# One-hots in sets of four, a table stream released through ScalarE, and later passes in a graph layer on one core

## Chip, cores and metric

One NeuronCore of a Trainium2 chip. The time is device microseconds for one execution of the kernel; the median of three runs is given with the lowest and the highest.

## What is computed

A graph layer: 12500 nodes of 128 features, 200000 edges sorted by their destination, four edge types. The reference, cut to what matters:

```python
def _layernorm(x, axis=-1, eps=1e-05):
    m = jnp.mean(x, axis=axis, keepdims=True)
    v = jnp.var(x, axis=axis, keepdims=True)
    return (x - m) / jnp.sqrt(v + eps)
...
# for every edge e: h = relu(_layernorm(x))
# out = x + segment_sum over dst of (h[src[e]] @ W[type[e]] + b[type[e]])
```

The two comment lines put into words what the reference does with a loop over the four types. Destinations are drawn as 12500·u², so low node numbers have many edges and high ones few.

## The kernel before

**The table.** In the first 190 us the kernel loads `x` by spans, makes `h`, splits each value into three bf16 parts and writes them to `htab`, 12500 rows of 3 × 128 bf16, in DRAM (`first_part`, `second_part`, `third_part`). Edges are handled in chunks of 128. From then on there are two kinds of work, which share all engines.

**The sparse part.** 1003 chunks with few edges per destination are gathered: `gather` (L543) issues one indirect DMA per chunk from GpSimd, two chunks to a tile `hm` of the pool `rows` (18 buffers). VectorE makes a one-hot `oh` of destination and type for each chunk (L560); TensorE multiplies rows by one-hot, three matmuls a chunk (L577, `sum_up`), into a bank `ps` for four chunks; ScalarE evicts it as `sb` (L580). For each group of 16 chunks `weigh` (L595 to L604) applies the four matrices, and VectorE adds the result to a ring of output columns (L665), which is transposed and written out (L690 to L697).

**The dense part.** The first 512 chunks belong to a few thousand destinations with many edges. Here the kernel counts how often each source stands in the edges of each (destination, type) pair, and multiplies the whole table by the counts. Destinations come in *units* of three, their edges in *slots* of 128, 1167 slots in all; up to 27 units make a *batch*, 18 batches (`MANY`, `UB`).

- `count(vs, counts)`: for every slot VectorE makes two one-hots, `o1` (128 × 128, L947 or L951, source within a block, scaled so that the three destinations of a unit land in three bytes of one number) and `o2` (128 × 392, L952, block and type). TensorE multiplies them (L963) into a bank `pt` of `x_ps` (four buffers), and after the last slot of a unit ScalarE turns the bank into int32 `counts` (L966, 476 evictions). One-hots are made `AHEAD` = 8 slots ahead, in 12 buffers each.
- `multiply(vs, counts)`: reads the bytes of `counts` as fp8 numbers. SP streams the table, `HB` = 4 of its 98 columns (128 partitions × 384 bf16 each) to a load `hs` (L997, pool of 4 buffers, 25 loads a pass, 450 in all). For each column three matmuls, one for each part of `h`, accumulate in the bank `pa` (L1001, 294 a pass, 5292 in all), which has one buffer. After the last one ScalarE moves `pa` to `sd` (L1011), and `tail` applies the matrices (L1015).
- `dense_work()` runs `multiply` of batch n and `count` of batch n + 1 side by side: at each step the one with the least share done goes on, with `BEHIND` = 0.06 added to the pass. `pace()` says how much of the dense work stands beside each chunk of the sparse part.

**What sets the order.** From L1248 on the order of TensorE, VectorE and ScalarE is written out by hand (`tc.manual_schedule`): their instructions run in the order in which the Python program emits them. A tile that is taken again from its pool waits for the last reader of its buffer, by a semaphore of the reader's engine. SP and GpSimd issue their DMAs in their own order and wait, one after the other, for the buffer of each.

The main loop goes over groups of 16 chunks, and within one over `sum_up`'s steps; each step runs the dense work up to `pace`, then a share of the small VectorE jobs (`side`). `tails` are jobs that a pass leaves behind: `tail`, its additions, and `check_sums`, ten small VectorE instructions per batch that check the counts.

Of the kernel before, what the change touches and what calls it, by code (L numbers as in the profile page):

```python
# [35 lines left out]
F32 = mybir.dt.float32  # L36
BF16 = mybir.dt.bfloat16
# [11 lines left out]
P = 128  # L49
# [6 lines left out]
C0 = 512  # L56
UB = 27
MANY = 16
HB = 4
AHEAD = 8  # L60
HOTS = AHEAD + 4
BEHIND = 0.06
RING = 2048
OT = 4
HG = 2
# [8 lines left out]
def kernel(  # L74
# [449 lines left out]
    def gather_raw(k, by):  # L524
# [9 lines left out]
                held_by(one, by, "rows of x come while the table is made, spread over its blocks")  # L534
        return hm

    def gather(t0, g):
        got = []
        for h0 in range(0, g, HG):
            hm = hpool.tile([P, HG * D3], BF16, name="hm")  # L540
            for i in range(h0, min(h0 + HG, g)):
                at = (t0 + i) % (TURN * P)
                one = nc.gpsimd.indirect_dma_start(  # L543
                    out=hm[:, (i - h0) * D3 : (i - h0 + 1) * D3],
                    out_offset=None,
                    in_=htab,
                    in_offset=bass.IndirectOffsetOnAxis(ap=srcf[:, at : at + 1], axis=0),
                )
# [19 lines left out]
    def sum_up(t0, g, rows, oh, last):  # L568
        win = window_of(C0 + t0)
        K = NT * win  # L570
        sb = spool.tile([P, G * KM], F32, name="sb")[:, : G * K].rearrange("p (g t n) -> p g t n", g=G, t=NT)
        for i0 in range(0, g, SG):
            i1 = min(i0 + SG, g)
            ps = s_ps.tile([P, 512], F32, name="ps")[:, : SG * K].rearrange("p (i n) -> p i n", i=SG)
            for i in range(i0, i1):
                for c in range(3):
                    nc.tensor.matmul(ps[:, i - i0, :], rows(i, c), oh[:, i, :], start=(c == 0), stop=(c == 2))  # L577
                if i % HG and i + 1 < i1:
                    yield (i + 1) / g
            nc.scalar.copy(sb[:, i0:i1].rearrange("p g t n -> p g (t n)"), ps[:, : i1 - i0, :])  # L580
            yield i1 / g

        finish.append(weigh(t0, g, oh, sb, last))
# [348 lines left out]
            nc.scalar.copy(acc[:, a:z], pn[:, : z - a])  # L932


    def count(vs, counts):
        todo = []
        for i, u in enumerate(vs):
            of = slots_of(u)
            todo += [(i, c, by, n == 0, n == len(of) - 1) for n, (c, by) in enumerate(of)]
        made = {}  # L940

        def make(k):
            i, s, by, first, last = todo[k]
# [8 lines left out]
            nc.vector.tensor_scalar(o2[:, :NB], iota_n, hkT[:, s : s + 1], None, ALU.is_equal)  # L952
            made[k] = o1, o2

        done = 0
        for k, (i, s, by, first, last) in enumerate(todo):
            while done < min(k + 1 + AHEAD, len(todo)):
                make(done)
                done += 1
            o1, o2 = made.pop(k)  # L960
            if first:
                pb = x_ps.tile([P, NB + NT], F32, name="pt")
            nc.tensor.matmul(pb, o1, o2, start=first, stop=last)  # L963
            if last:

                nc.scalar.copy(counts[:, :, i * NT : (i + 1) * NT], pb.rearrange("p (b t) -> p b t", t=NT))  # L966
            yield (k + 1) / len(todo)
        def check_sums():
            n = len(vs)
            bi = sdp.tile([P, UB], I32, name="bi")  # L970
            nc.vector.tensor_copy(bi[:, :n], counts[:, NW, : n * NT].rearrange("p (i t) -> p i t", t=NT)[:, :, 0])
            bb = sdp.tile([P, 3, UB], I32, name="bb")
            nc.vector.tensor_single_scalar(bb[:, 0, :n], bi[:, :n], 255, op=ALU.bitwise_and)
            nc.vector.tensor_single_scalar(bb[:, 2, :n], bi[:, :n], 16, op=ALU.arith_shift_right)
            nc.vector.tensor_single_scalar(bi[:, :n], bi[:, :n], 8, op=ALU.arith_shift_right)
            nc.vector.tensor_single_scalar(bb[:, 1, :n], bi[:, :n], 255, op=ALU.bitwise_and)
            bf = sdp.tile([P, 3, UB], F32, name="bf")
            nc.vector.tensor_copy(bf[:, :, :n], bb[:, :, :n])
            top = sdp.tile([P, 2], F32, name="top")
            nc.vector.tensor_reduce(top[:, 0:1], bf[:, :, :n], AX.XY, ALU.max)  # L980
            nc.vector.tensor_reduce(top[:, 1:2], bf[:, :, :n], AX.XY, ALU.add)
            nc.vector.tensor_max(most, most, top[:, 0:1])
            nc.vector.tensor_add(held, held, top[:, 1:2])

        tails.append(check_sums)

    tails = []

    def multiply(vs, counts):
        nu = len(vs)  # L990
# [3 lines left out]
        for j0 in range(0, NW, HB):  # L994
            j1 = min(j0 + HB, NW)
            hs = hsp.tile([P, HB, D3], BF16, name="hs")
            nc.sync.dma_start(hs[:, : j1 - j0, :], htab.rearrange("(p j) f -> p j f", j=NW)[:, j0:j1, :])  # L997
            for j in range(j0, j1):
                of = counts[:, j, : nu * NT * 4].rearrange("p (v m) -> p m v", m=4)[:, :3, :]
                for c in range(3):  # L1000
# [246 lines left out]
    o2s = op2.tile([P, HOTS, NB + NT], BF16, name="o2")  # L1247
    nc.vector.memset(o2s[:, :, NB:], 1.0)  # L1248
# [23 lines left out]
    for gi, (t0, g) in list(enumerate(zip(starts, sizes)))[RAW:]:  # L1272
# [16 lines left out]
        for j, part in enumerate(sum_up(t0, g, *now, gi >= FULL)):  # L1289
# [27 lines left out]
        if work is None and not dense_out:  # L1317
            while tails:
                tails.pop(0)()
            dense_out = True  # L1320
            assert goes[0] < gi

# [161 lines left out]
```

## Time and profile before

| | us |
|---|---|
| median of 3 runs | 1678.33 |
| lowest, highest | 1674.64, 1681.06 |
| profiled execution | 1684.81 |
| its span in the profile | 1683.1 |

The profile is of one execution. Engines: PE is TensorE's matmul, PEld its weight load, which overlaps; DVE is VectorE, ACT ScalarE, POOL GpSimd, SP SyncE (SPq is its DMA queue). Lines such as L963 are lines of the kernel. A group of instructions is shown as line, engine, operation, output <- inputs and count, then busy time and the mean ns of one, then idle time of the engine ahead of it and what ended most of that. The chain is followed back from the last instruction to what released each step; "issue" in it is time in which the engine waited for nothing that the profile shows. The waits' columns are the time in total (us), the times, and the longest. The timeline and the chain in order of time give start (us), duration (us) and what ran. The stretches give the length, then busy us and the number of instructions for each engine, the clock that TensorE was granted, the share of the DMA engines and GB/s.

### The profile page before, as it was taken

The page shows a single profiled execution, that of the slowest core. Times are in us where ns is not written, and L with a number is a line of the kernel's source. Part 1 is how long each engine was busy: PE and PEld are TensorE (multiplying, and loading weights), DVE is VectorE, ACT ScalarE, POOL GpSimd, SP SyncE. Part 2 cuts the span into 40 slices and gives each one's busy share as a digit, 9 for nine tenths or more (in the row PEclk, how much of TensorE's full clock was granted, in tenths as well). Part 3 has the DMA queues.
Part 4 walks back from the last instruction along what each step waited for, and adds up shares of the span by engine and source line. Part 5 has one row for each costly group of instructions (what it writes and reads, how often), then busy time and mean ns, then how long its engine had stood idle before and what let it go on. Part 6 is the DMA issues. An engine that isn't in the chain of part 4 may idle for free.

```text
span 1683.1 us, 32652 instructions
## 1 busy us (share of the span) xinstructions
PE 1420.6 (84%) x10984; PEld 926.8 (55%) x10984; DVE 1033.9 (61%) x5305; ACT 445.3 (26%) x1095; POOL 1026.0 (61%) x1078
## 2 busy tenths in 40 slices
PE   3768589898889988888989888988888988898885
PEld 1336366555565556555656555655555555565554
DVE  7880677665766566576647566656654756565244
ACT  5593231222212122212221222122222222222111
POOL 7436666666666566666665666666656666666561
PEclk9875699999999999999999999999999999999997
DMA  7543376766666666666666666666656666666662
GB/s 225 158 155 82 88 233 207 205 199 193 201 190 194 190 196 191 203 193 183 197 194 183 185 196 183 191 201 187 188 165 193 203 187 191 181 194 186 198 185 68
DMA packets 157498, 308.92 MB, mean 184 GB/s; under 512 B 28202, under 2 KB 81116, under 8 KB 157325
## 3 DMA queue, kind: packets, MB, share of 16 engines
q1 hardware_dynamic: 107645, 204.99, 40.3%
q0 software_dynamic: 49680, 101.81, 21.3%
q8 instruction: 86, 1.41, 0.4%
q14 instruction: 87, 0.71, 0.1%
HBM read 290.65 MB, written 16.04 MB: 182 GB/s over the span
## 4 chain that ended last, share of the span: by engine, by line
PE 77%; issue 10%; DVE 5%; another core or an unknown queue 3%; ACT 2%; DMA 2%; SPq 1%; DVEq 0%; ACTq 0%
PE pa L1001 45%; PE pt L963 12%; PE ps L577 7%; PE py L604 6%; PE pt L1015 1%; DMA hs<-htab 1%; PE ps L634 1%; PE py L595 1%; PE pt L690 1%; DVE stt L439 1%; ACT h L460 1%; DVE o L952 1%; DMA hm<-in_x_dram 1%; DVE oh L560 1%
## 5 line engine op out<-in xcount | busy, mean ns | idle before, releaser
L543 POOL DMA_INDIRECT hm<-htab,srcT x1003 | 970.2, 967 | 580.3 <-issue 225.4
L1001 PE MATMUL pa<-counts,hs 128*128 128x324 fp8e4 (+1 forms) x5292 | 976.1, 305 | 112.9 <-issue 95.8
L1001 PEld LDWEIGHTS <-hs 128*128 128x128 bf16 x5292 | 494.2, 97 | 396.0 <-issue 167.9
L963 PE MATMUL pt<-o,o 128*128 128x396 bf16 x1167 | 383.5, 338 | 45.8 <-issue 39.1
L952 DVE TENSOR_SCALAR o<-iota_n,hkT 128x392 bf16<-128x392 f16 x1167 | 386.2, 331 | 14.0 <-PE pa L1001 5.5
L966 ACT CAST counts<-pt 128x396 int32<-128x396 f32 x476 | 229.4, 494 | 506.5 <-PE pt L963 204.4
L560 DVE TENSOR_SCALAR oh<-iota_b,keyT 128x56 bf16<-128x56 bf16 (+8 forms) x1003 | 169.3, 259 | 265.4 <-PE pt L963 88.1
L580 ACT COPY sb<-ps 128x224 f32<-128x224 f32 (+8 forms) x251 | 99.6, 397 | 531.2 <-PE pt L963 182.9
L665 DVE TENSOR_TENSOR ring<-ring,py 128x14 f32 (+7 forms) x976 | 167.5, 172 | 102.5 <-issue 21.5
L577 PE MATMUL ps<-oh,hm 128*128 128x56 bf16 (+8 forms) x3009 | 192.2, 197 | 29.3 <-issue 28.6
L951 DVE TENSOR_SCALAR o<-iota,loT 128x128 bf16<-128x128 bf16 x644 | 169.7, 264 | 75.2 <-PE pt L963 27.8
L577 PEld LDWEIGHTS <-hm 128*128 128x128 bf16 x3009 | 164.7, 98 | 89.5 <-issue 43.7
L951 DVE TENSOR_SCALAR o<-iota,loT,byT 128x128 bf16<-128x128 bf16 x417 | 136.1, 326 | 81.4 <-PE pt L963 40.9
L963 PEld LDWEIGHTS <-o 128*128 128x128 bf16 x1167 | 113.2, 98 | 95.3 <-issue 43.8
L604 PE MATMUL py<-sb,wsb 128*128 128x224 f32 (+7 forms) x488 | 128.6, 404 | 3.5 <-issue 3.2
L604 PEld LDWEIGHTS py<-sb,wsb 128*128 128x128 f32 x488 | 87.3, 191 | 28.5 <-issue 6.8
L527 POOL DMA_INDIRECT hx<-in_x_dram,srcT x48 | 50.2, 1045 | 39.4 <-DVE stt L439 13.9
L599 ACT CAST cnt<-py 128x224 bf16<-128x224 f32 (+7 forms) x61 | 24.0, 394 | 96.4 <-PE pt L963 29.2
L460 ACT ACTIVATE h<-hm,nmrt,rstdt 128x128 f32<-128x128 f32 x98 | 42.8, 495 | 3.5 <-DMA hm<-in_x_dram 2.6
L489 PE MATMUL ps<-h,ident 128*128 128x384 f32 (+1 forms) x34 | 18.1, 618 | 17.7 <-ACT h L460 14.6
L947 DVE TENSOR_SCALAR o<-iota,loT 128x128 bf16<-128x128 bf16 x106 | 26.8, 253 | 8.5 <-remote 4.2
L1015 PE MATMUL pt<-sd,wsb 128*128 128x81 f32 (+1 forms) x144 | 25.4, 334 | 2.7 <-ACT sd L1011 2.7
(234 smaller groups left out, 623.2 us busy)
## 6 DMA issues: line engine op xcount, KB each, us to landing
hs<-htab SPq DMA_DIRECT2D x432, 384.0 KB
hm<-htab,srcT POOLq DMA_INDIRECT x1003
htab<-h SPq DMA_DIRECT2D x32, 288.0 KB
xo<-in_x_dram SPq DMA_DIRECT2D x23, 256.0 KB
out_dram<-xo SPq DMA_DIRECT2D x23, 256.0 KB
hm<-in_x_dram SPq DMA_DIRECT2D x18, 192.0 KB
hs<-htab SPq DMA_DIRECT2D x18, 192.0 KB
hm<-in_x_dram SPq DMA_DIRECT2D x14, 168.0 KB
```

Source lines behind the costliest of these rows:

```text
L460: return nc.scalar.activation(h, xt(k), AF.Relu, bias=nmr[:, k : k + 1], scale=rstd[:, k : k + 1]).ins
L543: one = nc.gpsimd.indirect_dma_start(out=hm[:, (i - h0) * D3 : (i - h0 + 1) * D3], out_offset=None, in_=htab, in_offset=bass.IndirectOffse ...
L560: nc.vector.tensor_scalar(oh[:, i, :], iota_b[:, :K], keyf[:, at : at + 1], None, ALU.is_equal)
L577: nc.tensor.matmul(ps[:, i - i0, :], rows(i, c), oh[:, i, :], start=(c == 0), stop=(c == 2))
L580: nc.scalar.copy(sb[:, i0:i1].rearrange("p g t n -> p g (t n)"), ps[:, : i1 - i0, :])
L604: nc.tensor.matmul(py[:, :g, :], wsb[:, t, :], sb[:, :g, t, :], start=False, stop=(t == NT - 1))
L665: nc.vector.tensor_tensor(to, to, of(i), ALU.add)
L951: nc.vector.tensor_scalar(o1, iota_1, loT[:, s : s + 1], by, ALU.is_equal, ALU.mult)
L952: nc.vector.tensor_scalar(o2[:, :NB], iota_n, hkT[:, s : s + 1], None, ALU.is_equal)
L963: nc.tensor.matmul(pb, o1, o2, start=first, stop=last)
L966: nc.scalar.copy(counts[:, :, i * NT : (i + 1) * NT], pb.rearrange("p (b t) -> p b t", t=NT))
L1001: nc.tensor.matmul(pa[:, : 3 * nu * NT].rearrange("p (m v) -> p m v", m=3), hs[:, j - j0, c * D : (c + 1) * D], of, start=(j == 0 and c == 0),
```

## The change

- `HB` 4 → 5: 98 columns make 20 loads a pass, 360 in all, of 491,520 bytes for 393,216; `hs` has 3 buffers for 4 (`STREAM`).
- A load of `hs` no longer waits for the matmul that last read its buffer. It waits for the first eviction of counts (ScalarE) that was emitted after that matmul, if there is one by then (`left_at`, `by_blocks`); otherwise for the matmul as before.
- One-hots in sets of four slots (`SLOTS`), four sets in all (`SETS`). The first one-hot of a set waits for the last counting matmul of the set four before; the first counting matmul of a set waits for the set's last one-hot. `o2` is made ahead of `o1`. Two sets are complete, and the next one grows by one slot per counting matmul.
- `BEHIND` 0.06 → 0.15.
- The pool `rows` has 16 buffers for 18, and a gather waits until all buffers of its block of four chunks have been read (`readers`, `BLOCK`).
- `check_sums` does one of its steps per chunk of the sparse part and no longer all in one place.

The diff, cut to its core:

```diff
@@ -56,10 +56,13 @@
 C0 = 512
 UB = 27
 MANY = 16
-HB = 4
-AHEAD = 8
-HOTS = AHEAD + 4
-BEHIND = 0.06
+HB = 5
+SLOTS = 4
+SETS = 4
+STREAM = 3
+ROWS = 16
+BLOCK = 4
+BEHIND = 0.15
 RING = 2048
 OT = 4
 HG = 2
@@ -230,7 +233,7 @@
     flag = const.tile([P, 1], I32, name="flag")
 
     mid = ExitStack()
-    hpool = mid.enter_context(tc.tile_pool(name="rows", bufs=18))
+    hpool = mid.enter_context(tc.tile_pool(name="rows", bufs=ROWS))
     opool = mid.enter_context(tc.tile_pool(name="onehots", bufs=2))
     spool = mid.enter_context(tc.tile_pool(name="typed", bufs=2))
     x_ps = mid.enter_context(tc.tile_pool(name="x_ps", bufs=4, space=PSUM))
@@ -534,10 +537,15 @@
                 held_by(one, by, "rows of x come while the table is made, spread over its blocks")
         return hm
 
+    taken = [0]
+    readers = []
+
     def gather(t0, g):
         got = []
         for h0 in range(0, g, HG):
             hm = hpool.tile([P, HG * D3], BF16, name="hm")
+            taken[0] += 1
+            left = taken[0] + (min(h0 // BLOCK * BLOCK + BLOCK, g) - h0 - 1) // HG - 1 - ROWS
             for i in range(h0, min(h0 + HG, g)):
                 at = (t0 + i) % (TURN * P)
                 one = nc.gpsimd.indirect_dma_start(
@@ -548,6 +556,8 @@
                 )
                 if i == h0 and gates and t0 + i >= SOON:
                     held_by(one, gates.pop(0), "the first rows come while the slots are made, not ahead of them")
+                if left >= 0:
+                    held_by(one, readers[left], "a block of rows comes when all of its buffers are free")
             got.append(hm)
         return lambda i, c: got[i // HG][:, (i % HG * 3 + c) * D : (i % HG * 3 + c + 1) * D]
 
@@ -574,7 +584,9 @@
             ps = s_ps.tile([P, 512], F32, name="ps")[:, : SG * K].rearrange("p (i n) -> p i n", i=SG)
             for i in range(i0, i1):
                 for c in range(3):
-                    nc.tensor.matmul(ps[:, i - i0, :], rows(i, c), oh[:, i, :], start=(c == 0), stop=(c == 2))
+                    one = nc.tensor.matmul(ps[:, i - i0, :], rows(i, c), oh[:, i, :], start=(c == 0), stop=(c == 2))
+                if i % HG == HG - 1 or i == g - 1:
+                    readers.append(one.ins)
                 if i % HG and i + 1 < i1:
                     yield (i + 1) / g
             nc.scalar.copy(sb[:, i0:i1].rearrange("p g t n -> p g (t n)"), ps[:, : i1 - i0, :])
@@ -932,59 +944,93 @@
             nc.scalar.copy(acc[:, a:z], pn[:, : z - a])
 
 
+    left_at = []
+    by_blocks = [0]
+    released = []
+
     def count(vs, counts):
         todo = []
+        sets = []
         for i, u in enumerate(vs):
             of = slots_of(u)
-            todo += [(i, c, by, n == 0, n == len(of) - 1) for n, (c, by) in enumerate(of)]
-        made = {}
-
-        def make(k):
-            i, s, by, first, last = todo[k]
-            o1 = op1.tile([P, P], BF16, name="o1")
-            o2 = o2s[:, k % HOTS, :]
-            if by == 1.0:
-                nc.vector.tensor_scalar(o1, iota_1, loT[:, s : s + 1], None, ALU.is_equal)
-            else:
-                if by is None:
-                    by = byT[:, (s - PAIRS) // 2 : (s - PAIRS) // 2 + 1]
-                nc.vector.tensor_scalar(o1, iota_1, loT[:, s : s + 1], by, ALU.is_equal, ALU.mult)
-            nc.vector.tensor_scalar(o2[:, :NB], iota_n, hkT[:, s : s + 1], None, ALU.is_equal)
-            made[k] = o1, o2
-
+            of = [(i, c, by, n == 0, n == len(of) - 1) for n, (c, by) in enumerate(of)]
+            todo += of
+            for one in [of[n : n + SLOTS] for n in range(0, len(of), SLOTS)]:
+                if not sets or len(sets[-1]) + len(one) > SLOTS:
+                    sets.append([])
+                sets[-1] += one
+        before = len(released)
+        released.extend(None for _ in sets)
+
+        def make(n):
+            at = before + n
+            o1 = op1.tile([P, SLOTS, P], BF16, name="o1")
+            o2 = o2s[:, at % SETS]
+            for k, (i, s, by, first, last) in enumerate(sets[n]):
+                one = nc.vector.tensor_scalar(o2[:, k, :NB], iota_n, hkT[:, s : s + 1], None, ALU.is_equal)
+                if k == 0 and at >= SETS:
+                    held_by(one, released[at - SETS], "a set of slots has been counted as a whole")
+                if by == 1.0:
+                    one = nc.vector.tensor_scalar(o1[:, k], iota_1, loT[:, s : s + 1], None, ALU.is_equal)
+                else:
+                    if by is None:
+                        by = byT[:, (s - PAIRS) // 2 : (s - PAIRS) // 2 + 1]
+                    one = nc.vector.tensor_scalar(o1[:, k], iota_1, loT[:, s : s + 1], by, ALU.is_equal, ALU.mult)
+                yield o1[:, k], o2[:, k], one.ins
+
+        making = []
+        made = []
         done = 0
-        for k, (i, s, by, first, last) in enumerate(todo):
-            while done < min(k + 1 + AHEAD, len(todo)):
-                make(done)
+        for n, of in enumerate(sets):
+            while len(making) < min(n + 3, len(sets)):
+                making.append(make(len(making)))
+                made.append([])
+            for m in range(n, min(n + 2, len(sets))):
+                made[m] += list(making[m])
+            for k, (i, s, by, first, last) in enumerate(of):
+                if n + 2 < len(sets) and len(made[n + 2]) < len(sets[n + 2]):
+                    made[n + 2].append(next(making[n + 2]))
+                o1, o2, _ = made[n][k]
+                if first:
+                    pb = x_ps.tile([P, NB + NT], F32, name="pt")
+                one = nc.tensor.matmul(pb, o1, o2, start=first, stop=last)
+                if k == 0:
+                    held_by(one, made[n][-1][2], "a set of slots is counted when all of it is made")
+                if k == len(of) - 1:
+                    released[before + n] = one.ins
+                if last:
+                    one = nc.scalar.copy(counts[:, :, i * NT : (i + 1) * NT], pb.rearrange("p (b t) -> p b t", t=NT))
+                    left_at.append((by_blocks[0], one.ins))
                 done += 1
-            o1, o2 = made.pop(k)
-            if first:
-                pb = x_ps.tile([P, NB + NT], F32, name="pt")
-            nc.tensor.matmul(pb, o1, o2, start=first, stop=last)
-            if last:
-
-                nc.scalar.copy(counts[:, :, i * NT : (i + 1) * NT], pb.rearrange("p (b t) -> p b t", t=NT))
-            yield (k + 1) / len(todo)
+                yield done / len(todo)
+            made[n] = None
+
         def check_sums():
...
-        tails.append(check_sums)
+        checks.append(check_sums())
 
     tails = []
+    checks = []
 
     def multiply(vs, counts):
         nu = len(vs)
@@ -994,7 +1040,11 @@
         for j0 in range(0, NW, HB):
             j1 = min(j0 + HB, NW)
             hs = hsp.tile([P, HB, D3], BF16, name="hs")
-            nc.sync.dma_start(hs[:, : j1 - j0, :], htab.rearrange("(p j) f -> p j f", j=NW)[:, j0:j1, :])
+            one = nc.sync.dma_start(hs[:, : j1 - j0, :], htab.rearrange("(p j) f -> p j f", j=NW)[:, j0:j1, :])
+            free = [by for n, by in left_at if n > by_blocks[0] - STREAM]
+            if free and by_blocks[0] >= STREAM:
+                held_by(one, free[0], "the buffer of the stream is free")
+            del left_at[: len(left_at) - len(free)]
             for j in range(j0, j1):
                 of = counts[:, j, : nu * NT * 4].rearrange("p (v m) -> p m v", m=4)[:, :3, :]
                 for c in range(3):
@@ -1005,6 +1055,8 @@
                         start=(j == 0 and c == 0),
                         stop=(j == NW - 1 and c == 2),
                     )
+                if j + 1 == j1:
+                    by_blocks[0] += 1
                 if j + 1 < NW:
                     yield (j + 1) / NW
         sd = sdp.tile([P, 3 * UB * NT], F32, name="sd")
...
-    op1 = counting.enter_context(tc.tile_pool(name="op1", bufs=AHEAD + 4))
+    op1 = counting.enter_context(tc.tile_pool(name="op1", bufs=SETS))
...
-    hsp = counting.enter_context(tc.tile_pool(name="hsp", bufs=4))
+    hsp = counting.enter_context(tc.tile_pool(name="hsp", bufs=STREAM))
...
             for f in late:
                 f()
+            if checks and next(checks[0], None) is None:
+                checks.pop(0)
```

More of the change, by code (lines that the diff above doesn't have):

```diff
@@ L971, in check_sums @@
             nc.vector.tensor_copy(bi[:, :n], counts[:, NW, : n * NT].rearrange("p (i t) -> p i t", t=NT)[:, :, 0])
+            yield True
             bb = sdp.tile([P, 3, UB], I32, name="bb")
@@ L974, in check_sums @@
             nc.vector.tensor_single_scalar(bb[:, 2, :n], bi[:, :n], 16, op=ALU.arith_shift_right)
+            yield True
             nc.vector.tensor_single_scalar(bi[:, :n], bi[:, :n], 8, op=ALU.arith_shift_right)
             nc.vector.tensor_single_scalar(bb[:, 1, :n], bi[:, :n], 255, op=ALU.bitwise_and)
+            yield True
             bf = sdp.tile([P, 3, UB], F32, name="bf")
             nc.vector.tensor_copy(bf[:, :, :n], bb[:, :, :n])
+            yield True
             top = sdp.tile([P, 2], F32, name="top")
@@ L981, in check_sums @@
             nc.vector.tensor_reduce(top[:, 1:2], bf[:, :, :n], AX.XY, ALU.add)
+            yield True
             nc.vector.tensor_max(most, most, top[:, 0:1])
             nc.vector.tensor_add(held, held, top[:, 1:2])
-        tails.append(check_sums)
+        checks.append(check_sums())
     tails = []
+    checks = []
     def multiply(vs, counts):
@@ L1244 @@
     sdp = counting.enter_context(tc.tile_pool(name="sdp", bufs=1))
-    op1 = counting.enter_context(tc.tile_pool(name="op1", bufs=AHEAD + 4))
+    op1 = counting.enter_context(tc.tile_pool(name="op1", bufs=SETS))
     op2 = counting.enter_context(tc.tile_pool(name="op2", bufs=1))
-    o2s = op2.tile([P, HOTS, NB + NT], BF16, name="o2")
-    nc.vector.memset(o2s[:, :, NB:], 1.0)
-    hsp = counting.enter_context(tc.tile_pool(name="hsp", bufs=4))
+    o2s = op2.tile([P, SETS, SLOTS, NB + NT], BF16, name="o2")
+    nc.vector.memset(o2s[:, :, :, NB:], 1.0)
+    hsp = counting.enter_context(tc.tile_pool(name="hsp", bufs=STREAM))
     raw_sums = outp.tile([P, OT, D], F32, name="xo").rearrange("p j d -> p (j d)")[:, : RAW * G * win_raw]
@@ L1319 @@
                 tails.pop(0)()
+            for check in checks:
+                for _ in check:
+                    pass
             dense_out = True
```

## Prediction

> **What bounds the kernel now.** I read the shares by engine and the chain first, then the costliest groups, the stretches, one switch between two passes, and the waits of SP.
>
> ```profile
> PE 1420.6 (84%) x10984; PEld 926.8 (55%) x10984; DVE 1033.9 (61%) x5305; ACT 445.3 (26%) x1095; POOL 1026.0 (61%) x1078
> PE 77%; issue 10%; DVE 5%; another core or an unknown queue 3%; ACT 2%; DMA 2%; SPq 1%; DVEq 0%; ACTq 0%
> L1001 PE MATMUL pa<-counts,hs 128*128 128x324 fp8e4 (+1 forms) x5292 | 976.1, 305 | 112.9 <-issue 95.8 <-ACT sd L1011 9.0 <-ACT sb L580 3.7
> ```
>
> TensorE (PE) carries 77% of the chain; a further 10%, 0.10 × 1683.1 = 170 us, is "issue": PE stands still and the profile shows nothing that it waits for. The largest group, the multiplication of the table by the counts (L1001), is late by 95.8 us for such "issue" and hardly for anything named. No other engine is full: VectorE (DVE) 61%, GpSimd (POOL) 61%, ScalarE (ACT) 26%.
>
> Is this standing still caused by the many waits and signals of the counting? The change removes those, so I compared a stretch that has no counting matmul (L963) with one in mid-loop. Columns: length, busy time and instructions of PE, weight loads, DVE, ACT, POOL; clock; DMA. The last two rows count L963 alone (PE and weight loads).
>
> ```profile
> 300.00:350.00 50.00, 44.22 (x371) 29.89 (x370) 34.51 (x179) 10.91 (x29) 32.16 (x33) 1.00 0.68 203
> 1586.00:1633.00 47.00, 41.33 (x330) 27.05 (x329) 20.75 (x121) 4.91 (x11) 29.22 (x32) 1.00 0.67 201
> 300.00:350.00 50.00, 13.62 (x43) 4.11 (x43) 1.00 0.68 203
> 1586.00:1633.00 47.00, 0.00 (x0) 0.00 (x0) 1.00 0.67 201
> ```
>
> PE is busy 44.22/50 = 88.4% with counting and 41.33/47 = 87.9% without. Between, the chain shows short stops at even distances:
>
> ```profile
> 1433.66 0.93 issue
> 1445.67 0.96 issue
> 1457.68 0.97 issue
> ```
>
> One of about 0.95 us each 12 us. They come where nothing waits, so I take them to go with the number of rows PE runs, not with its waits. The change leaves that number as it is (10984 matmuls).
>
> The longest stops lie at the switches between passes (a pass is 98 table columns × 3 matmuls for one batch; 18 passes, 17 switches). Chain and timeline:
>
> ```profile
> 331.94 1.41 issue
> 722.54 3.15 issue
> 802.41 2.54 issue
> 1388.34 1.72 issue
> 1559.78 4.56 issue
> ...
> 800.11 1.45 PE L1001 MATMUL pa<-counts,hs 128*128 128x324 fp8e4 x9
> 801.41 0.83 PE L963 MATMUL pt<-o,o 128*128 128x396 bf16 x4
> 804.46 0.45 ACT L1011 ACTIVATE sd<-pa 128x324 f32<-128x324 f32 x1
> 804.95 0.59 PE L1001 MATMUL pa<-counts,hs 128*128 128x324 fp8e4 x3 [2.54 <-issue]
> ```
>
> The last matmul of the old pass ends at 801.56. ScalarE starts to read `pa` only at 804.46, **2.9 us** later: so long PE's signal takes to be seen. The new pass starts at 804.95 in the same bank, so each switch pays signal, eviction and restart. The table stream isn't missed there; its four buffers were filled during the old pass.
>
> **The change part by part.**
>
> *Stream (`hs`): 5 columns a load for 4, three buffers for four, release through ScalarE.* Rows that price a load: SP's issue, how often PE waits for one, SP's own waits, ScalarE's waits for the counting, the queue, and loads that were on the chain.
>
> ```profile
> L997 SPq DMA_DIRECT2D hs<-htab x450: 319/320/1452, 116.8 to 1628.3; - x150
> ...
> PEld L1001: 5.7, 8
> SPq L997 <- PE pt L963: 420.3, 150, 8.2
> SPq L997 <- PE pa L1001: 268.5, 88, 5.7
> ACT counts L966 <- PE pt L963: 204.4, 110, 5.3
> L966 ACT CAST counts<-pt 128x396 int32<-128x396 f32 x476 | 229.4, 494 | 506.5 <-PE pt L963 204.4
> q1 hardware_dynamic: 107645, 204.99, 40.3%
> 232.20 4.08 DMA hs<-htab
> 238.42 4.33 DMA hs<-htab
> 1264.78 3.84 DMA hs<-htab
> ```
>
> Today SP waits 2.8 to 3.1 us for a release (420.3/150, 268.5/88) and PE still waits 5.7 us in all for the stream: the lead covers it. After the change a load waits for the first eviction of counts (L966) that is emitted after its buffer's last reader. Mid-pass that takes the signal of the counting matmul to ScalarE, 204.4/110 = 1.86 us, the eviction 0.49, SP's issue 0.32 and the load, 3.84 by the last of the chain's rows: 6.5 us.
>
> (A) *First load of a pass.* `BEHIND` .06 → .15 ends counting 15% of a pass before the pass ends. No eviction is left there to release buffers, so the last three blocks run out, and the first three loads of the next pass all wait for the first eviction of the new head. That head has 15% of some 65 slots = 10 counting matmuls before the first L1001 (today 4). At the switch above: 801.56, + 0.67 for the 2 to 6 counting matmuls of the first unit (the chain has four in 0.67), + 2.9 signal, + 0.49 eviction, + 0.32 issue, + 3.84 load = 809.78, against 804.95: 4.83 later. Of that, 6 counting matmuls more stand in the head that are done elsewhere today, 6 × 0.167 = 1.0. Net **3.8 us × 16 passes = +61**. Bounds: at the queue's own rate (204.99 MB in 40.3% of 1683.1 us = 302 GB/s) 491,520 bytes take 1.63 us, which gives 1.6 × 16 = +26; the longer load 4.33 by the size 5/4 is 5.4 us, 5.4 × 16 = +86. I take the middle, because 3.84 is a load that PE really waited for.
>
> [...]
>
> (B) *Fourth load of a pass.* It is emitted after the first block (15 L1001) and waits for the next eviction. In the new order 42 to 62 weight-load/matmul rows, 21 to 31 pairs, stand in 12 of 16 passes between that eviction's last matmul and the load's first use. By the first stretch above a pair is 50/371 = 0.135 us, so 2.8 to 4.2 us stand against 1.86 + 0.49 + 0.32 + 3.84 = 6.5: 2.3 to 3.7 us late if nothing else has delayed PE, and PE's own stop falls into it. I take 2.0 × 12 = **+24** (0 to +44).
>
> (C) *The other 300 or so loads.* The order puts a median of 47 pairs there, 47 × 0.135 = 6.3 us against 6.5: just in time. I take **0**, since 0.2 us late every fourth us or so falls where PE stops for 0.95 us anyway. If those stops don't absorb it, 0.3 to 0.9 us each: up to +270. The stream's start, where the chain holds loads at 232.20 and 238.42, has the same waits with larger loads: 0 to +4.
>
> (D) *Payback.* After a long wait the next even stop comes late. For 16 + 12 waits I take one stop of 0.95 back each, **−27** (0 to −27).
>
> *One-hots in sets of four, rows by blocks of four chunks.* Same VectorE instructions, same matmuls. In the two instruction streams fewer instructions wait for PE: one-hots on VectorE 837 → 202, gathers on GpSimd 484 → 243, stream loads 443 → 81 (274 now wait for ScalarE). By the stretch without counting this is worth **0**; the bound below is rival 1. An added wait, the first counting matmul of a set for the set's last one-hot, stands in front of everything behind it on PE; two sets are made ahead, 8 to 12 slots:
>
> ```profile
> PE pt L963 <- DVE o L952: 2.5, 6, 0.7
> L952 DVE TENSOR_SCALAR o<-iota_n,hkT 128x392 bf16<-128x392 f16 x1167 | 386.2, 331 | 14.0 <-PE pa L1001 5.5
> L543 POOL DMA_INDIRECT hm<-htab,srcT x1003 | 970.2, 967 | 580.3 <-issue 225.4 <-PE pt L963 126.4 <-PE ps L577 77.1
> ```
>
> Eight slots lie 8 × 50/43 = 9.3 us of PE's order ahead of use (43 counting matmuls in the first stretch), VectorE is 61% busy, and PE waits 2.5 us in all for it today. **0** (to +10). Rows: POOL's chain, 1003 × (0.967 + 0.306 for each step without a wait, 225.4 us in 736 of them) = 1277 us, is shorter than the loop of some 1430 us (205 to 1640); 16 buffers hold 32 chunks for 36, of which up to 3 wait for their block, which leaves a lead of 29 × 1430/1003 = 41 us. **0** (to +5 in stage 1). The check sums move from one burst of ten small VectorE instructions per batch to one step per chunk: **0**, hidden by the same slack.
>
> **Sum.** 61 + 24 − 27 = +58 on the profiled execution's 1684.8 us: 1743. The median of the runs shown is 1678.33, a factor of 0.9962: **1736 us**. Term bounds: 26 + 0 − 27 below, 86 + 44 + 0 above without (C): 1677 to 1808.
>
> **Rivals.**
> 1. *Fewer signals, fewer stops: faster.* The 170 us of "issue" less 17 switches of about 2.2 (the first four of the five rows above: 8.8/4) = 37 leave 133. If PE's waits and signals feed them, and the change leaves a third fewer of the waits (3766 → 2560 on PE's instructions), −43; signals that are then seen at once take −16 from the switches and most of (A) with it (26 − 10): 1678 − 43 = **1635**. For it: L1001's lateness has no named cause, and the signal takes 2.9 us. Against it: 87.9% busy without counting. [...] Chance 0.26.
> 2. *Late loads only replace the even stops: the same.* The stop that PE would have had falls into each late load, (A) at its lower bound is paid by (D): 26 − 27, 1678 ± 8. Chance 0.08.
> 3. *Forecast*, A and B decide: 1690 to 1790. Chance 0.53.
> 4. *Every load is late* (C): three buffers hold 15 columns, and the chain signal → eviction → issue → load of 6.5 us stands against 6.3. From 0.3 us late it shows: 300 × 0.3 = 90 on top, **1826** and more. Chance 0.13.
>
> Two runs here can be told apart from about 0.5%, 8 us. Faster 0.26, same 0.08, slower 0.66. The range reaches down to rival 1 and up over most of (A)'s and (B)'s bounds: **1632 to 1808**; left out are rival 4 and what lies below rival 1.
>
> **What would show it.** (A): at the 16 switches after the first, "DMA hs<-htab" or ACT counts appear in the chain ahead of L1001, 3 to 5 us after the head; at present only 1264.78 has one mid-loop. (B): a second stop one block into the pass. (C): many loads in PE's waits, busy share under 85% in 300:350. Rival 1: issue below 8%, PE's share above, the even stops gone or further apart than 12 us. The forecast is wrong if signals come sooner than 1.9 us with fewer of them, since A, B and C all rest on that delay.

## The result and the profile after

The changed kernel takes 1764.19 us (median of 4 runs, 1762.44 to 1770.37), the kernel before beside it 1676.49 us (1673.64 to 1681.06): a ratio of 1.0527, 95% interval 1.0489 to 1.0565, 88 us slower. The forecast was 1736, 58 us slower, with a range of 1632 to 1808.

The three groups of runs below found the kernel before at 1708, 1709 and 1405 us, so a run is compared only with the runs of before beside it, and the third group is also a second condition of the chip, in which TensorE's stops without a named cause are missing (0.2 us in a0, 73.9 in the three matmul groups of the first profile of the same kernel).

The page of the kernel after, with the same rows as before (L1001 is now L1051, L963 is L996):

```profile
PE 1453.7 (83%) x10984; PEld 941.0 (53%) x10984; DVE 1013.8 (58%) x5305; ACT 447.4 (25%) x1095; POOL 1032.2 (59%) x1078
PE 53%; DMA 15%; issue 14%; DVE 6%; another core or an unknown queue 6%; ACT 5%; SPq 1%; DVEq 0%; ACTq 0%
L1051 PE MATMUL pa<-counts,hs 128*128 128x324 fp8e4 (+1 forms) x5292 | 988.4, 313 | 174.8 <-DMA hs<-htab 137.7
L996 PE MATMUL pt<-o,o 128*128 128x396 bf16 x1167 | 377.3, 346 | 30.9 <-issue 15.0
```

TensorE's share of the chain falls from 77% to 53%; DMA rises from 2% to 15%, ScalarE from 2% to 5%. "issue" rises too, from 10% to 14%, but it no longer means TensorE's stops alone: the chain now runs through the stream's loads, and a piece such as the 10.61 us shown with the head below stands ahead of a load. The table stream, for which TensorE hardly ever waited, now keeps L1051 waiting for 137.7 us. The waits of the kernel after, by TensorE, by SP's queue and by ScalarE (us in total, times, longest):

```profile
PE pa L1051 <- DMA hs<-htab: 137.7, 85, 4.9
PE pa L1051 <- issue: 32.5, 59, 1.5
PE ps L587 <- issue: 26.4, 43, 1.9
PE pt L996 <- issue: 15.0, 19, 5.5
```

```profile
SPq L1043 <- ACT counts L1002: 661.9, 158, 14.9
```

```profile
ACT counts L1002 <- PE pt L996: 292.0, 169, 7.4
```

158 of SP's loads now wait 661.9/158 = 4.2 us each for an eviction of counts, up to 14.9 us. For lack of a named cause ("issue") L1001 waited 95.8 us in the kernel before, and by the same view of it the two other matmul groups:

```profile
PE pt L963 <- issue: 39.1, 34, 10.9
PE ps L577 <- issue: 28.6, 48, 3.8
```

That is 163.5 us together; now it is 32.5 + 15.0 + 26.4 = 73.9. So 90 us of stops without a named cause went while 138 us of waits for the stream came.

Which loads are these? A pass has 294 L1051, 15 to a load, so each of the 85 waits in the trace has a place in its pass. 14 of them are for the first load of a pass (51.1 us), 12 for the fourth (23.7 us) and 59 for all the others (62.9 us).

One more term shows in the first row: the same 10984 matmuls keep TensorE busy for 1453.7 us, 33.1 more than before. The budget of the span, 1683.1 to 1760.6: +138 stream, +33 slower matmuls, −90 stops = +81, for a measured +77.5.

One head of a pass, from the timeline of the kernel after, and the load in it from the chain:

```profile
826.16 1.45 PE L1051 MATMUL pa<-counts,hs 128*128 128x324 fp8e4 x9
827.65 0.83 PE L996 MATMUL pt<-o,o 128*128 128x396 bf16 x4
830.56 0.67 PE L996 MATMUL pt<-o,o 128*128 128x396 bf16 x3 [0.37 <-issue]
831.62 0.45 ACT L1063 ACTIVATE sd<-pa 128x324 f32<-128x324 f32 x1
832.22 0.49 ACT L1002 CAST counts<-pt 128x396 int32<-128x396 f32 x1 [0.15 <-remote]
836.04 0.99 PE L1051 MATMUL pa<-counts,hs 128*128 128x324 fp8e4 x3 [4.82 <-DMA hs<-htab]
```

```profile
822.12 10.61 issue
832.74 3.26 DMA hs<-htab
```

The old pass ends at 827.61. The sums are evicted 4.0 us later, the first counts at 832.22, the load starts behind them and lands at 836.00. The forecast's chain is all there: signal, two evictions, issue, load; 8.4 us in all, and the forecast had 8.2 (809.78 − 801.56). But this head is the longest of the 14 that wait for a load. Over all 14 the load is issued 2.7 us behind the old pass's last matmul and lands 3.5 us after that, 6.2 us in all; the forecast had 4.1 and 4.2. Behind the wait shown, the first three matmuls of the new pass take 0.99 us for 0.59. The clock in the stretches around (length, PE, PEld, DVE, ACT, POOL, clock, DMA share, GB/s), and one mid-loop:

```profile
822.00:827.00 5.00, 5.00 (x45) 3.35 (x43) 4.49 (x27) 0.37 (x1) 2.99 (x4) 1.00 0.62 201
832.00:836.00 4.00, 0.00 (x0) 0.00 (x0) 1.91 (x11) 0.56 (x2) 3.09 (x4) 0.75 0.66 214
836.00:839.50 3.50, 3.46 (x15) 2.66 (x15) 0.00 (x0) 0.00 (x0) 0.39 (x1) 0.50 0.74 292
841.00:845.00 4.00, 4.00 (x34) 2.67 (x33) 4.00 (x28) 0.42 (x2) 3.08 (x4) 1.00 0.19 55
300.00:350.00 50.00, 40.14 (x303) 25.53 (x302) 27.85 (x150) 8.67 (x22) 28.05 (x29) 0.90 0.55 175
```

The granted clock falls during the wait: 0.75 over 832 to 836 is 1.00 and then 0.50 for half of it, from 834.0. It stays at 0.50 until 840.8 by the trace's clock record, 4.8 us behind the restart, and is 1.00 again from there; over the span it is 0.922 for 0.95 before. The clock falls 2.8 us after TensorE's last matmul here (830.56 + 0.67 = 831.23).

In 300 to 350, 40.14/50 = 80% is busy for 88% before. That stretch is an extreme: in 1200 to 1250 the same view has 44.70 us busy after and 42.78 before.

### The profile page after: what moved, and what is told of

Same layout as the page of the kernel before. It is cut to its first block, busy times and chain, and to the rows that moved or that the text cites. A ratio compares the mean times of both kernels' runs of the same rounds, so it can differ in the third digit from the quotient of the medians.

```text
span 1760.6 us, 32298 instructions
## 1 busy us (share of the span) xinstructions
PE 1453.7 (83%) x10984; PEld 941.0 (53%) x10984; DVE 1013.8 (58%) x5305; ACT 447.4 (25%) x1095; POOL 1032.2 (59%) x1078
## 4 chain that ended last, share of the span: by engine, by line
PE 53%; DMA 15%; issue 14%; DVE 6%; another core or an unknown queue 6%; ACT 5%; SPq 1%; DVEq 0%; ACTq 0%
PE pa L1051 30%; DMA hs<-htab 13%; PE pt L996 9%; PE py L616 5%; PE ps L587 4%; ACT counts L1002 2%; PE pt L1067 1%; DVE oh L570 1%; DVE o L970 1%; DVE o L978 1%; ACT sb L592 1%; PE py L607 1%; PE pt L702 1%; DMA out_dram<-xo 1%
## 5 line engine op out<-in xcount | busy, mean ns | idle before, releaser
L1051 PE MATMUL pa<-counts,hs 128*128 128x324 fp8e4 (+1 forms) x5292 | 988.4, 313 | 174.8 <-DMA hs<-htab 137.7
L1051 PEld LDWEIGHTS <-hs 128*128 128x128 bf16 x5292 | 498.1, 99 | 468.0 <-DMA hs<-htab 176.3
L996 PE MATMUL pt<-o,o 128*128 128x396 bf16 x1167 | 377.3, 346 | 30.9 <-issue 15.0
L587 PE MATMUL ps<-oh,hm 128*128 128x56 bf16 (+8 forms) x3009 | 191.4, 199 | 32.1 <-issue 26.4
L978 DVE TENSOR_SCALAR o<-iota,loT 128x128 bf16<-128x128 bf16 x644 | 172.7, 268 | 0.0
L996 PEld LDWEIGHTS <-o 128*128 128x128 bf16 x1167 | 114.4, 100 | 85.4 <-issue 29.5
L978 DVE TENSOR_SCALAR o<-iota,loT,byT 128x128 bf16<-128x128 bf16 x417 | 141.3, 339 | 0.0
L1011 DVE COPY bi<-counts 128x27 int32<-128x27 int32 (+1 forms) x18 | 3.6, 203 | 100.8 <-ACT counts L1002 66.6
L1067 PEld LDWEIGHTS pt<-sd,wsb 128*128 128x128 f32 x144 | 28.8, 279 | 2.2 <-ACT sd L1063 0.4
```

Source lines behind the costliest of these rows:

```text
L587: one = nc.tensor.matmul(ps[:, i - i0, :], rows(i, c), oh[:, i, :], start=(c == 0), stop=(c == 2))
L978: one = nc.vector.tensor_scalar(o1[:, k], iota_1, loT[:, s : s + 1], by, ALU.is_equal, ALU.mult)
L996: one = nc.tensor.matmul(pb, o1, o2, start=first, stop=last)
L1051: nc.tensor.matmul(pa[:, : 3 * nu * NT].rearrange("p (m v) -> p m v", m=3), hs[:, j - j0, c * D : (c + 1) * D], of, start=(j == 0 and c == 0),
```

## The experiments

My theory: the release through ScalarE is late, above all at the head of a pass; the rest of the change is worth about nothing. Rivals: the larger loads in fewer buffers; the later start; fewer signals that make TensorE faster. Ratios are to the kernel before in the same group, with 95% intervals.

### First group: one part of the change undone, or alone (before: 1708.1 us)

**e1_pe_release**: the stream released by TensorE again.

```diff
-            if free and by_blocks[0] >= STREAM:
-                held_by(one, free[0], "the buffer of the stream is free")
```

> The changed kernel with the stream's buffers released by TensorE's last reader again; all else as changed (5 columns, 3 buffers, sets of four, blocks of rows, BEHIND 0.15). Theory 1 (the release through ScalarE is late, above all at the head of a pass): the 137.7 us for which TensorE waits for the stream fall below 20, the time goes back to 1665 to 1690. Theory 2 (larger loads in fewer buffers are what starves the stream): the waits stay above 70 us, the time above 1725. Theory 3 (fewer signals make TensorE faster, and the stream hides it): about 1640. Theory 4 (the later start of passes): above 1725.

Measured 1722.25 us, ratio 1.0081 (1.006 to 1.0102). TensorE's wait for the stream:

```profile
PE pa L1049 <- DMA hs<-htab: 12.2, 13, 1.8
```

5 columns, 3 buffers and 0.15 are all still there, and 137.7 us have become 12.2. By the ratios of the two groups (the changed kernel itself wasn't run in this one) the release accounts for some 4.5 of the 5.3%, so theories 2 and 4 fall as the main cause, and theory 3 with them: without the starved stream the kernel isn't faster than before. The 0.8% that stay are at the upper edge of theory 1's range.

**e2_behind06**: `BEHIND = 0.15` → `0.06`.

> The changed kernel with BEHIND 0.06 as before. Theory 1: release through ScalarE is late in every place where few evictions stand ahead of a load; by the new order the loads 0 to 6 of a pass are then late in place of the first alone, in sum as much (226 us of lateness without carrying over, against 223): 1745 to 1770. Theory 4 (the later start is the cause): 1665 to 1700. My prediction's term A alone (no eviction in the last 15% of a pass): some 40 to 50 us less, 1710 to 1725.

Measured 1769.45 us, ratio 1.0352 (1.0328 to 1.0375), between the two expectations (1.041 to 1.056 and 1.020 to 1.029 as ratios to 1676).

```profile
PE pa L1051 <- DMA hs<-htab: 134.7, 94, 4.5
```

The waits for the stream are the same in sum, 134.7 us for 137.7, in more and shorter pieces. By place, the 51.1 us at the first loads have become 0.7: with evictions up to the pass's end the first load is in time, which shows what had made it late. Other loads are late instead: 17.7 us at the second, 24.8 at the fourth, 91.5 at the rest. So the later start alone isn't the cause, and 0.06 isn't the cure. How much of the 1.75 points between this run and the first result is the chip, this group doesn't tell.

**e4_act_4x4**: `HB = 5` → `4`, `STREAM = 3` → `4`.

> The changed kernel with 4 columns a load and 4 buffers as before, release through ScalarE and BEHIND 0.15 kept. Theory 1: the head of a pass stays as it is (terms A and B), the late loads of mid-pass (some 31 us by the trace) go, since the order puts a median of 118 rows for 94 between release and use: 1725 to 1745. Theory 2 (size and number of buffers are the cause): 1665 to 1695.

Measured 1783.73 us, ratio 1.0432 (1.0403 to 1.0461); my range was 1.029 to 1.041.

```profile
PE pa L1051 <- DMA hs<-htab: 106.7, 48, 11.5
```

Half as many waits, but longer ones. By place: 66.6 us at the first loads, 21.6 at the fifth (the first one issued inside the pass, with four buffers) and 18.5 at all others, which have 62.9 us in the changed kernel (my expectation had put them at 31). So size and number of the buffers are not the main cause (theory 2 had 0.993 to 1.011), but they are part of what makes the other loads late.

**e3_sets_rows_only**: `HB = 4`, `STREAM = 4`, `BEHIND = 0.06`, and the release as in e1.

> The changed kernel with the stream and BEHIND as before (4 columns, 4 buffers, released by TensorE, 0.06): the sets of four one-hots, the blocks of rows and the spread check sums alone. Theory 1: these are worth nothing, 1670 to 1685. Theory 3 (rival 1 of the prediction, fewer signals): 1625 to 1650.

Measured 1725.96 us, ratio 1.0091 (1.006 to 1.0122): neither. These parts cost something. A head in its timeline:

```profile
403.78 0.33 DVE L1011 COPY bi<-counts 128x27 int32<-128x27 int32 x1 [6.57 <-ACT counts L1002]
405.16 0.77 DVE L677 TENSOR_TENSOR ring<-ring,py 128x12 f32 x4 [1.05 <-issue]
405.85 0.32 DVE L970 TENSOR_SCALAR o<-iota_n,hkT 128x392 bf16<-128x392 f16 x1
407.70 0.54 PE L996 MATMUL pt<-o,o 128*128 128x396 bf16 x2 [1.97 <-DVE o L978]
```

VectorE reaches the copy that starts the check sums, waits 6.57 us for the last eviction of counts, and only then makes the new batch's first one-hots; TensorE waits 1.97 us until four slots of them are there. In the switch before (the kernel before, 800 to 805), the next batch's one-hots stood ahead of that copy, and the first counting matmul needed one slot.

### Second group: the remaining parts one by one (before: 1708.66 us)

**c0_before_again**: no edit.

> The kernel before, for a profile from the same chip as the runs beside it. Half-speed matmuls and single stops as in the first profile: issue 10% of the chain, waits of TensorE for the stream under 5 us.

Measured 1705.38 us; issue is 13% of the chain here:

```profile
PE 75%; issue 13%; DVE 5%; ACT 2%; another core or an unknown queue 2%; DMA 2%; POOL 1%; DVEq 0%; SPq 0%; ACTq 0%; POOLq 0%
```

**g1_rows_only**: the kernel before with `bufs=18` → `16` for the rows and

```diff
+                if left >= 0:
+                    held_by(one, readers[left], "a block of rows comes when all of its buffers are free")
```

> The kernel before with 16 buffers of rows released by blocks of four chunks, and nothing else. Theory S (what is left over without the release through ScalarE, 0.8 to 0.9%, comes from the sets): ratio 0.998 to 1.002. Theory R (it comes from the rows): 1.006 to 1.011. Rival 1 of the prediction (fewer signals): 0.99.

Measured 1716.8 us, ratio 1.0048 (1.0028 to 1.0068). The pages of c0 and of g1:

```profile
PE 1424.5 (84%) x10984; PEld 924.6 (54%) x10984; DVE 1035.0 (61%) x5305; ACT 444.8 (26%) x1095; POOL 1030.5 (60%) x1078
```

```profile
PE 1434.9 (84%) x10984; PEld 929.3 (54%) x10984; DVE 1030.1 (60%) x5305; ACT 443.2 (26%) x1095; POOL 1028.3 (60%) x1078
```

The blocks of rows, with the two buffers fewer, cost 8 us. The same matmuls keep TensorE busy 10.4 us longer, at a granted clock of 0.942 over the span for 0.953. That doesn't explain the 8 us, though: g2 below has the same busy time, 1434.9 us, at 0.943 and loses nothing. No wait for a gather shows either, so the cause stays open.

**g2_sets_only**: e3 without the blocks of rows (the two lines of g1 taken out).

> Sets of four one-hots and spread check sums, with 16 buffers of rows released one by one; stream and BEHIND as before. Theory S (the first counting matmul of a batch waits for a whole set, and on VectorE the copy that starts the check sums now stands ahead of that set): ratio 1.006 to 1.011, waits of TensorE for VectorE's one-hots at the head of each pass, about 2 us each. Theory R: 0.998 to 1.002.

Measured 1705.22 us, ratio 0.998 (0.9966 to 0.9995). Theory S as I put it falls: in this group the sets cost nothing in sum, though the waits at the heads are there (TensorE waits 11.4 us for one-hots between 250 and 1600). With the blocks of rows on top (e3, in the first group) it is 1.0091, more than the two alone give.

**g3_behind15_only**: the kernel before with `BEHIND = 0.15`.

> The kernel before with BEHIND 0.15 and nothing else. If the ten counting matmuls of the head fill the hole that the eviction of the sums leaves between two passes: 6 more of 0.167 us in 16 holes, 16 us less, ratio 0.99. If the even stops take the place of what is filled, as in rival 2: 0.998 to 1.002. If the later start itself costs: above 1.004.

Measured 1704.06 us, ratio 0.9968 (0.9949 to 0.9986): a gain of about 5 us, a third of the 16 that filling the holes promised; the rest of what is filled comes back as stops elsewhere or isn't filled.

### Third group: the forecast's terms taken away one by one (before: 1405.38 us)

The chain's shares in a0, which is the changed kernel; the same kernel had issue at 14% in the result above. A profile of the kernel before was not taken in this condition.

```profile
PE 74%; DMA 15%; DVE 4%; ACT 4%; issue 1%; SPq 0%; DVEq 0%; POOL 0%; ACTq 0%; POOLq 0%
```

**a0_after_again**: the changed kernel.

> The changed kernel, beside the runs that take its terms away one by one. Ratio to before 1.045 to 1.057.

Measured 1526.09 us, ratio 1.0857 (1.0834 to 1.0881), 120.7 us slower: far outside what I expected. My reading is that in this condition nothing covers a late load: TensorE's stops without a named cause, 73.9 us in the first profile of this kernel, are 0.2 us here. By place, its waits for the stream are 45.7 us at the first loads, 21.4 at the fourth and 16.0 at the others.

**h1_head3_by_pe** and **h2_head4_by_pe**: the first three, or four, loads of a pass released by TensorE.

```diff
-            if free and by_blocks[0] >= STREAM:
+            if free and by_blocks[0] >= STREAM and by_blocks[0] % -(-NW // HB) >= 3:
```

> The changed kernel, but the first three loads of each pass wait for TensorE's last reader of their buffer as before, not for ScalarE. This takes away term A of the prediction alone. Theory A decides (61 us as forecast): ratio 1.010 to 1.022. A is 44 us, as the stops of TensorE at first loads in the trace after sum to: 1.022 to 1.032. Term C decides (late loads all through the pass): above 1.035. If a late load is only passed on to the next one, because ScalarE is late in any case: above 1.035 too, with the stops moved to loads 1 to 5.

> The same with the first four loads of each pass released by TensorE: terms A and B are both gone, C is left. By A 61, B 24: 1.002 to 1.010. By A 44, B 20: 1.012 to 1.020. If C decides: above 1.03.

Measured: h1 1463.89 us, ratio 1.0412 (1.039 to 1.0433); h2 1435.09 us, ratio 1.0222 (1.02 to 1.0244). Both ratios lie above what I gave for A and B, and by its letter the line "above 1.035" would speak for C. But they start from 1.0857 and not from 1.05, so the steps tell the terms. a0 − h1, the first loads: **62.2 us**. h1 − h2, the fourth load: **28.8 us**. h2 − before, all else: 29.7 us. TensorE's row of the page and its wait for the stream, first of a0, then of h1 and of h2:

```profile
PE 1383.4 (90%) x10984; PEld 928.0 (61%) x10984; DVE 1014.8 (66%) x5305; ACT 460.0 (30%) x1095; POOL 1036.2 (68%) x1078
```

```profile
PE pa L1051 <- DMA hs<-htab: 83.1, 49, 4.7
```

```profile
PE 1358.7 (93%) x10984; PEld 913.4 (63%) x10984; DVE 1011.4 (69%) x5305; ACT 460.0 (31%) x1095; POOL 1031.3 (71%) x1078
```

```profile
PE pa L1051 <- DMA hs<-htab: 37.0, 37, 2.7
```

```profile
PE 1349.0 (94%) x10984; PEld 909.9 (63%) x10984; DVE 1013.6 (71%) x5305; ACT 459.8 (32%) x1095; POOL 1036.3 (72%) x1078
```

```profile
PE pa L1051 <- DMA hs<-htab: 17.8, 26, 2.9
```

Each step has two parts. First loads: 83.1 − 37.0 = 46.1 us of waits, 2.9 a pass, and 24.7 us of TensorE's busy time, the same matmuls at a granted clock of 0.947 over the span for 0.967; together 70.8 of the 69.6 us by which the profiled spans differ. Fourth load: 19.2 + 9.7 = 28.9 of 28.2, at 0.967 for 0.974. So about a third of what a late load costs here is paid after it has landed, if the busy time that goes with each step is the half clock behind its waits, as in the head shown. One head in a0, then one in h1:

```profile
729.29 1.45 PE L1051 MATMUL pa<-counts,hs 128*128 128x324 fp8e4 x9
730.78 0.44 ACT L1063 ACTIVATE sd<-pa 128x324 f32<-128x324 f32 x1 [0.92 <-PE pa L1051]
731.97 0.49 ACT L1002 CAST counts<-pt 128x396 int32<-128x396 f32 x1 [0.74 <-PE pt L996]
736.47 0.99 PE L1051 MATMUL pa<-counts,hs 128*128 128x324 fp8e4 x3 [3.58 <-DMA hs<-htab]
```

```profile
694.41 1.45 PE L1051 MATMUL pa<-counts,hs 128*128 128x324 fp8e4 x9
695.90 0.44 ACT L1063 ACTIVATE sd<-pa 128x324 f32<-128x324 f32 x1 [0.92 <-PE pa L1051]
698.22 0.59 PE L1051 MATMUL pa<-counts,hs 128*128 128x324 fp8e4 x3
```

With ScalarE the new pass begins 736.47 − 730.74 = 5.7 us behind the old, and at half speed (0.99 us for three, at a clock of 0.50); with TensorE 698.22 − 695.86 = 2.4 us, and three take 0.59.

**h3_sets_behind15**: sets, spread check sums and 0.15 with 16 buffers of rows one by one, and the stream as before.

> Sets of four, spread check sums, 16 buffers of rows released one by one, BEHIND 0.15, and the stream as before (4 columns, 4 buffers, TensorE). The two parts that alone gave 0.998 and 0.997 together: 0.990 to 0.996, since with 0.15 the check sums' copy no longer stands ahead of the next batch's first set. If each only takes the other's gain (the same hole between two passes): 0.997 to 1.001.

Measured 1415.7 us, ratio 1.0072 (1.0058 to 1.0085), neither of the two. Both parts had gained 0.2 and 0.3% in the second group; here together they cost 10.3 us, so of the 29.7 us that h2 is still behind, 19.4 belong to what h2 has and h3 hasn't: larger loads in fewer buffers, ScalarE's release from the fifth load on, and the blocks of rows. Why the two parts cost something here stays open; TensorE waits about as long for its one-hots between 250 and 1600 as in g2:

```profile
PE pt L994 <- DVE o L976: 10.6, 12, 1.8
```

No kernel here beats the one before in both conditions: g3 leads by 0.3% in the second group and wasn't tried in the third.

## Why the prediction was right

The direction, the mechanism at the first and fourth loads and the range are right. That the sum is near is partly luck, because its terms miss by more than the sum does. The two traces of the first pair tell the terms apart: where TensorE stands still, and for how long (after less before, us; the 16 switches are those with counting matmuls in the head).

| term | forecast | first pair |
|---|---|---|
| A, standing still at the 16 switches | 61 | 30 (34 → 64) |
| B, waits for the fourth loads | 24 | 24 |
| C, waits for the other loads | 0 | 63 |
| D, all other stops | −27 | −72 |
| slower matmuls | not in the sum | 33 |
| together | 58 | 78 |

D is what is left of the spans' difference of 77.5 us. Sets and rows have no row of their own; what they cost lies in D and in the slower matmuls. By the medians the change costs 88 us.

*Where the stream restarts (A): right in place, too large for the first pair.* The heads take 6.2 us from the old pass to the landed load where I had 8.2. The signal comes sooner: the sums' eviction begins 1.1 us behind the pass's last matmul on average over the 17 switches, 2.7 us in the kernel before. Sooner signals were what I had named as the sign that the forecast is wrong; together with a shorter load (3.5 us for 4.2, issue included) they halved A, and other terms made up for it. That fewer signals are the reason isn't shown: in g2, which has fewer too, it is 3.0 us. In the third group taking A away is worth 62.2 us, but this is not the 61 of the forecast: h1 keeps the ten counting matmuls in the head, so by my working it takes away 4.83 us a pass, 77 us. The profiles split it into 46.1 us of waits and 24.7 of slower matmuls, a term that my sum didn't have at all. That the two numbers agree is luck.

*The fourth load (B), right.* Forecast 24 us from 12 passes; the first pair has 12 waits, 23.7 us. In the third group it is 28.8, 19.2 of it waits.

*The other loads (C), the largest miss.* I took 0, and 59 of them are late in the first pair, 1.1 us each. The sign that I had named for it came: many loads in TensorE's waits, and 80% busy in 300 to 350. The margin that I had worked out, 6.3 us against 6.5, was right to call it close, wrong to round it to nothing. Its 1.86 us for the signal was also misread: 204.4/110 is how long ScalarE stood idle ahead of a counting eviction, not how long a signal takes. In the third group, where signals come at once (0.04 us in the head of a0 shown), the same loads have 16.0 us of waits (a0), and h2, with A and B gone, 17.8 us in all.

*Payback (D), right in kind, too small.* Forecast −27, and some −72 in the first pair: by my reading a wait takes the place of stops that would have come anyway. In the kernel before, TensorE restarts at 804.95 behind the 2.54 us of the switch shown, and its next stop of 0.3 us or more ends at 828.64, 23.7 us later; from there on they follow each other after some 6 us (834.56, 840.61, 846.73, 852.76). The two conditions give a second view, 88 us slower where those stops are and 121 where they aren't, −33 in sum; but the signals differ between them as well, and this is read from two groups, not from one edit.

*Sets and rows, not settled.* I took 0 with 0 to +15. Blocks of rows alone cost 8 us (g1), the sets nothing in the second group (g2), both together 0.9% (e3), and sets with the later start 10 us in the third (h3). "Two sets are made ahead" doesn't hold at the head of a batch, where none is, and with 0.06 the check sums' first copy blocks VectorE there; TensorE's waits of 11 us show it, the time of g2 doesn't.

*Rival 1, fewer signals: out as a gain.* g2 has the sets' fewer signals with the stream as before (1820 increments by TensorE in its trace for 2649 in c0's), and gains 0.2%; the interval ends at 0.34%. The mechanism isn't excluded by this, and no run here shows what a signal costs TensorE: its stops without a named cause in the three matmul groups are 148 us in g2's profile for 175 in c0's, and 10.4 us of slower matmuls (1434.9 us busy for 1424.5) and new waits (11.4 us for one-hots) take most of that back. *Rival 2* (late loads only replace stops) holds for part of them: D is 72 us for 138 of waits. *Rival 4* (each load late) is not seen as stated, 85 waits of 360 loads, but C's 63 us are not far from the 90 that it began with.

## What to carry over

Price a release by the whole way to the next use: signal, the releasing engine's own queue, issue, transfer. A stand-in for the last reader that is usually early enough is latest where its own work pauses, here at the head of each pass; and where the margin is close to nothing, price it at many small waits and not at zero. Then add what a wait leaves behind: in the heads shown TensorE restarted at a clock of 0.50, and its slower matmuls are about a third of the cost in the third group (24.7 of 70.8 us, 9.7 of 28.9).

## What the runs showed of the hardware

The stops without a named cause go with the condition of the chip: for the changed kernel issue is 14% of the chain in the first profile and 1% in a0, and these stops of TensorE's three matmul groups are 73.9 us there and none here; the kernel before takes 1709 us in the second group and 1405 us in the third. Both of these groups ran on the chip numbered 3, so the chip alone doesn't decide it. With the stops goes the delay of TensorE's signal: in the heads shown `sd` begins 4.0 us after the pass's last matmul in the first profile of the changed kernel (831.62 against 827.61; 1.1 us on average over its 17 switches) and 0.04 us after it in a0 (730.78 against 730.74). The same change costs 5.3% in one condition and 8.6% in the other. What the stops are, no run here tells.

In both heads shown a wait of TensorE is followed by a lower clock: 4.82 us up to 836.04 in the kernel after, where the clock is 0.50 from 834.0 to 840.8, and 3.58 us up to 736.47 in a0, where it is 0.50 from 736 to 741.
